# A two-layer adaLN transformer on one core: the second layer's rows, convolution, sort, scatters and combination are put at other places in the order of work

## The chip, the cores and the metric

The program runs on one core of one Trainium2 chip. The core has five engines with a queue each: TensorE (PE, with its weight loads PEld), VectorE (DVE), ScalarE (ACT), GpSimd (POOL) and SyncE (SP), which here only starts transfers. An engine works its queue in order; what it waits for is another engine's result or a transfer. The metric is the device time of one execution in microseconds. The kernel before takes 1100.03 us (median of 3 runs, 1098.54 to 1102.29).

## The reference

Two layers work on x of 4 batches x 1024 rows x 256 columns, float32. In each, x gets a gated attention and then a gated mixture of experts, both on a layer norm that is scaled and shifted by a small modulation of c:

```python
h = _layernorm(x) * (1 + ca) + sa
x = x + ga * attention(h)
h = _layernorm(x) * (1 + cb) + sb
x = x + gb * experts(h)
```

Layer 0 has causal softmax attention (16 heads) and 16 experts with two chosen per row. Layer 1, which the change is about, has linear attention and 8 experts with one chosen:

```python
q, k, v = split(h @ w_qkv.T)                  # 16 heads of 16
q, k = norm(norm(relu(q) + eps) ** 3), norm(norm(relu(k) + eps) ** 3)
out = (q @ (k.T @ v)) / (q @ k.sum(rows) + eps)
conv = depthwise convolution of out over the rows, 3 taps, + b_dwc
attention = (out + conv) @ w_proj.T + b_proj

probs = softmax(h @ router_w + router_b)
experts = max(probs) * (h @ expert_w[argmax] + expert_b[argmax])
```

## The kernel before

All of x stays in SBUF (`k.x[b]`, 8 tiles of 128 rows). Layer 0 is untouched by the change, apart from a combination of its experts' results (`k.awaited`) that runs on into layer 1.

**Attention 1** (`attention1`) loops over b = 0 to 4. In turn b, the generators `front(b)` (norm, keys and values, queries) and `back(b - 1)` (output, convolution, projection, residual) are advanced by one `yield` each, turn by turn. A front takes 18 turns (23 where it computes its own statistics, b = 2 and 3), a back 13. A convolution takes two of them: ScalarE multiplies a 128x1024 half of the channels by the middle tap (L1597), VectorE adds the other two (L1601). Then four turns project (L1609) and add to x (L1614).

After each turn `k.around.step(pieces, rides)` (L44) lets other work in. `tasks` are generators whose yields are costs; `pieces` of cost are advanced per turn, by `pace` in sixths (L1622). `riders` are generators that are advanced `rides` times; they issue GpSimd's indirect transfers one by one. So what is around an instruction is set by the order of these calls. A planner then orders each engine's queue by readiness in that order; instructions given to `k.pin` keep their written order among themselves.

**Experts 1** (`Experts1`) sorts rows by expert. `PARTS` has three parts: batches 0 and 1, batch 2, batch 3. When a batch's back is done, `rows(b)` becomes a task: statistics, the normalised rows in two halves of four tiles (`routed_rows`, L1017; for batches 2 and 3 ScalarE alone does this, and scale and shift come later), a store to DRAM (`rows_in`), transposes, router logits. After a part's last batch, `sort(p)` finds each row's place and each tile's expert; then the rider `send(p)` loads rows (`hs`) and scatters them to `sorted1` with 8 indirect transfers per batch. Each scatter is tied (`paced`, L980) to the matmul that was last issued when it was written.

`run` (L1883) then goes through the pairs of sorted tiles, 11 for part 0 and 7 each for parts 1 and 2: load a pair (`xs`, up to five ahead, six buffers), transpose it (L1923), copy to SBUF (`xT`, L1927, or with scale and shift at L1930), multiply by its expert's weights (L1938), add the bias (L1944), gate (L1946), store to `results`. After each pair `around.step(2, 2)`. When a part's pairs are done, `combine(p)` becomes a task: it gathers result rows back (`ys`, L974, four ahead, six buffers), scales and adds them to x (L2002 to L2008 for part 0, L1996 for the others) and stores four tiles at a time to the output (L2010). Between, `count_sums` checks in three VectorE passes that all sums were in range (its tiles `good` take buffers of `xs`), and `out_of_bounds` reads the flag that decides whether a general version must run.

## Time and profile before

| what | us |
|---|---|
| median of the runs | 1100.03 |
| the profiled execution | 1087.63 |
| its span | 1085.8 |
| TensorE busy | 945.7 (87%) |
| VectorE busy | 620.4 (57%) |
| ScalarE busy | 602.5 (55%) |
| GpSimd busy | 336.0 (31%) |
| mean granted clock of TensorE | 0.955 |

Attention 1 begins at about 750 us of the span. The third turn of its loop (b = 2) is at about 830 to 885, the fourth at 885 to 937 and the fifth, the last back, at 937 to 970. The pairs of the experts follow until 1060. From there to 1085.8 the results of the last part are gathered and stored.

In the lines below, a form such as 128x512 is partitions by elements, x8 a number of instructions merged into one line, and a bracket the idle time of the engine before them with what ended it. A product appears as two records (ps_y x200 for 100 calls), a transpose as one (ps_xT x100 for 100). POOL's DMA_INDIRECT is the time in which GpSimd issues an indirect transfer, not the transfer itself.

### The profile page before, as it was taken

How to read it: one execution, taken by the hardware profiler on the slowest of the kernel's cores; microseconds unless marked ns; L12 is line 12 of the kernel's file. 1: busy time of each engine (PE TensorE's matmuls, PEld its weight loads, DVE VectorE, ACT ScalarE, POOL GpSimd, SP SyncE). 2: the span in 40 equal slices, each digit the busy share in tenths (PEclk: the TensorE clock that was granted, in tenths of full speed). 3: DMA queues.
4: the chain of work that ended last, by engine and by line, in shares of the span. 5: the costliest groups of instructions: out<-in, count | busy, mean ns of one | idle time of the engine just before them, and what ended most of it. 6: DMA issues, size and time to landing. Idle time of an engine off the chain costs nothing.

```text
span 1085.8 us, 18090 instructions
## 1 busy us (share of the span) xinstructions
PE 945.7 (87%) x6072; PEld 559.8 (52%) x6072; DVE 620.4 (57%) x1987; ACT 602.5 (55%) x959; POOL 336.0 (31%) x528
## 2 busy tenths in 40 slices
PE   4899999999999999889679989986997989858760
PEld 2434434443443434335568878874464656547550
DVE  5822235422465155413676767993899968564572
ACT  0368655765477555775555657766654745523430
POOL 2013211311232234663004615612550100553632
PEclk9999999999999999999899999998999899989875
DMA  6995000100010001552825556624223201458764
GB/s 206 358 346 179 1 1 6 40 1 1 1 64 1 1 30 54 201 215 78 317 88 170 197 177 189 196 75 144 67 65 148 88 2 39 141 170 264 240 205 130
DMA packets 97142, 132.89 MB, mean 122 GB/s; under 512 B 8536, under 2 KB 84216, under 8 KB 96528
## 3 DMA queue, kind: packets, MB, share of 16 engines
q1 hardware_dynamic: 84656, 97.27, 26.9%
q0 software_dynamic: 11776, 33.57, 9.9%
q8 instruction: 52, 0.85, 0.3%
q10 hardware_dynamic: 608, 0.79, 0.3%
q14 instruction: 50, 0.41, 0.1%
HBM read 67.85 MB, written 63.75 MB: 121 GB/s over the span
## 4 chain that ended last, share of the span: by engine, by line
PE 63%; DVE 19%; issue 5%; DMA 5%; ACT 4%; POOL 1%; SPq 1%; DVEq 0%; ACTq 0%; POOLq 0%
PE ps_s L388 13%; PE ps_av L453 12%; PE ps_qk L364 6%; PE ps_y L1312 5%; PE ps_h L1247 4%; PE ps_v L349 3%; PE ps_out L427 3%; PE ps_pr L1609 3%; PE ps_y L1938 3%; PE ps_q L1537 2%; PE ps_k L1511 2%; DVE y L1601 2%; DMA ys<-results,index 2%; PE ps_lnT L1057 1%; DVE st L1258 1%
## 5 line engine op out<-in xcount | busy, mean ns | idle before, releaser
L396 ACT ACTIVATE pT<-ps_s 128x1024 f32<-128x1024 f32 x288 | 279.3, 1022 | 169.7 <-PE ps_s L388 167.2
L399 POOL TENSOR_SCALAR_AFFINE_SELECT pT<-pT 128x256 f32<-128x256 f32 x256 | 104.2, 431 | 328.4 <-ACT pT L396 323.7
L388 PE MATMUL ps_s<-qT,kT 32*128 32x512 f32 (+3 forms) x1536 | 178.8, 523 | 0.1
L453 PE MATMUL ps_av<-pT,v 128*32 128x512 f32 (+3 forms) x1536 | 165.2, 497 | 9.4 <-DVE turned L411 5.6
L964 POOL DMA_INDIRECT sorted<-hs,index x96 | 96.2, 1002 | 144.9 <-PE ps_y L1312 73.0
L974 POOL DMA_INDIRECT ys<-results,index x96 | 102.7, 1070 | 119.0 <-DMA results<-y 43.6
L388 PEld LDWEIGHTS ps_s<-qT,kT 32*128 32x128 f32 x1536 | 74.5, 185 | 95.5 <-issue 72.8
L453 PEld LDWEIGHTS ps_av<-pT,v 128*32 128x32 f32 x1536 | 40.6, 108 | 104.0 <-issue 58.7
L1247 PE MATMUL ps_h<-w,xT 128*128 x352 | 82.1, 386 | 6.5 <-DVE mv L1259 3.8
L1312 PE MATMUL ps_y<-w,act 128*128 x352 | 83.7, 392 | 4.2 <-DVE rs_seed L84 2.8
L411 DVE STREAM_TRANSPOSE turned<-ps_av 128x512 f32<-128x512 f32 x32 | 22.8, 712 | 98.9 <-PE ps_av L453 98.6
L1312 PEld LDWEIGHTS ps_y<-w,act 128*128 128x128 f32 x352 | 67.7, 197 | 14.0 <-ACT act L1295 4.8
L1247 PEld LDWEIGHTS ps_h<-w,xT 128*128 128x128 f32 x352 | 66.2, 193 | 15.9 <-issue 4.2
L1295 ACT ACTIVATE act<-ps_hT,gain 128x128 f32<-128x128 f32 x176 | 63.6, 463 | 16.9 <-PE ps_hT L1286 16.8
L1270 ACT ACTIVATE hid<-hid,nmr,rstd 128x256 f32<-128x256 f32 x88 | 47.5, 603 | 39.4 <-DVE nmr L1263 39.2
L1511 PE MATMUL ps_k<-wqkv,hT 128*128 128x512 f32 x128 | 61.9, 603 | 3.6 <-DMA wqkv<-in_wqkv_dram 2.8
L1938 PE MATMUL ps_y<-we,xT 128*128 x200 | 53.0, 412 | 10.6 <-ACT xT L1930 8.4
L371 DVE COPY qT<-ps_qk 128x512 f32<-128x512 f32 x16 | 11.0, 688 | 81.8 <-PE ps_qk L364 81.8
L103 DVE BATCH_NORM_STATS2 ln_st<-x 128x6 f32<-128x256 f32 x128 | 49.2, 407 | 0.5
L1255 DVE TENSOR_TENSOR hid<-ps_h,b 128x256 f32<-128x256 f32 x88 | 33.9, 415 | 26.6 <-PE ps_h L1247 21.5
L1938 PEld LDWEIGHTS ps_y<-we,xT 128*128 128x128 f32 x200 | 38.2, 204 | 20.1 <-ACT xT L1930 11.6
L374 DVE TENSOR_SCALAR kT<-ps_qk,par 128x512 f32<-128x512 f32 x32 | 22.5, 745 | 37.0 <-PE ps_qk L364 37.0
(223 smaller groups left out, 1499.4 us busy)
## 6 DMA issues: line engine op xcount, KB each, us to landing
xs<-sorted SPq DMA_DIRECT2D x69, 256.0 KB, 3.8
results<-y SPq DMA_DIRECT2D x69, 256.0 KB, 3.0
sorted<-zero SPq DMA_DIRECT2D x2, 6016.0 KB, 20.1
rows_in<-h SPq DMA_DIRECT2D x16, 512.0 KB, 2.9
hs<-rows_in POOLq DMA_DIRECT2D x32, 256.0 KB, 3.5
w<-in_w_dram SPq DMA_DIRECT2D x8, 1024.0 KB, 11.3
x<-in_x_dram SPq DMA_DIRECT2D x4, 1024.0 KB, 6.5
b<-in_b_dram SPq DMA_DIRECT2D x2, 2048.0 KB
```

What stands on the lines that cost most here:

```text
L364: nc.tensor.matmul(ps, lhsT=w[:, cc, g * P : (g + 1) * P], rhs=hT[:, cc, hf * 512 : (hf + 1) * 512], start=cc == 0, stop=cc == CC - 1,)
L388: k.anchor = nc.tensor.matmul(pair[hh // 2][:, hh % 2, c0 : c0 + w], lhsT=kTs[o][rows, kb * P : (kb + 1) * P], rhs=qT[rows, q1 - w : q1], ...
L396: nc.scalar.activation(pT, ps, AF.Exp, scale=1.0 / L**0.5)
L399: nc.gpsimd.affine_select(out=pT[:, :, c0 : c0 + P], in_=pT[:, :, c0 : c0 + P], compare_op=ALU.is_ge, fill=0.0, base=0, pattern=[[0, 2], [ ...
L453: nc.tensor.matmul(po[32 * hh : 32 * hh + 32, 512 - w :], lhsT=vs[b % 2][:, kb, 8 * g + 2 * hh + o, :], rhs=exps[b, g, o, u][hh // 2][:, h ...
L964: i = self.k.nc.gpsimd.indirect_dma_start(out=buffer.ap, out_offset=bass.IndirectOffsetOnAxis(ap=index, axis=0), in_=rows, in_offset=None, ...
L974: self.paced(self.k.nc.gpsimd.indirect_dma_start(out=rows, out_offset=None, in_=buffer.ap, in_offset=bass.IndirectOffsetOnAxis(ap=index, a ...
L1247: mm = nc.tensor.matmul(ph[:, j], lhsT=xTs[i // 2][:, j, cc], rhs=w1[:, cc, bass.ds(at[i + j], C)], start=cc == 0, stop=cc == CC - 1,)
L1295: o = nc.scalar.activation(act[:, j, cc], pt[:, j, cc], AF.Gelu, bias=gain[:, 1, cc, t : t + 1], scale=gain[:, 0, cc, t : t + 1],)
L1312: mm = nc.tensor.matmul(po[:, j], lhsT=acts[i // 2][:, j, cc], rhs=w2[:, cc, bass.ds(at[i + j], C)], start=cc == 0, stop=cc == CC - 1,)
L1511: k.anchor = nc.tensor.matmul(ps, lhsT=hT[:, cc, t * P : (t + 1) * P], rhs=wqkv[:, cc, C:], start=cc == 0, stop=cc == CC - 1,).ins
L1938: k.anchor = nc.tensor.matmul(po[:, j], lhsT=xT[:, j, cc], rhs=self.we[:, cc, bass.ds(at[j], C)], start=cc == 0, stop=cc == CC - 1,).ins
```

## The change

- In turn b = 2, the tasks around begin after the first seven turns. The paces of b = 2 and b = 3 go from 6 to 8 and 9. Riders are advanced twice per turn from b = 3 on.
- Where ScalarE normalises alone (batches 2 and 3), both halves are normalised ahead of the transposes.
- The addition of 1 to the middle tap moves from the start of attention 1 to the first back.
- The last back convolves 511 and 513 columns, each as soon as its half of `o` is there, inside two turns that exist already; so it has 11 turns.
- During its turns 6 to 9, four pairs of part 0 are worked on (`beside`), in free buffers of `hT` and in PSUM of the fronts.
- In `run`, 3.5 pieces of the last batch's rows go ahead of the first pair; the rest of rows and sort are spread over the next seven pairs as 0, 2, 3.5, 2.5, 0, 2, 2 pieces. Three rides follow each pair.
- The last part's scatters go to the head of the riders and are not tied to a matmul.
- The gathers are riders of their own, with 24 buffers; the combination of part 0 begins four pairs before the end, the others after all gathers are issued. One more of its instructions is pinned.
- `count_sums` yields after each pass, one pass per pair of part 0; its tiles take the buffers of `out`.

The core of the diff (in the new methods, `tiles_of` is as before, but for the PSUM and SBUF it takes from `k.bank` and `self.space`, and pins on its first transpose, its copies and its first matmul):

```diff
-        good = pool.tile([P, 8 * B * H], F32, tag="xs", name="good", bufs=6)
+        good = pool.tile([P, 8 * B * H], F32, tag="out", name="good")
         count_within(k, good, rec, low, high, k.good[:, i : i + 1])
+        yield
...
-        self.paced(i)
+        if not at_once:
+            self.paced(i)
...
     h = yield from normalised(0)
+    second = (yield from normalised(1)) if scale is None else None
...
+            if b == B - 1:
+                for _ in convolve(o, y, *((0, N // 2 - 1), (N // 2 - 1, N))[q]):
+                    pass
             yield
...
+        if b < B - 1:
+            yield from convolve(o, y, 0, N)
...
-        pace = (6, 8, 6, 6, 12)[b]
+        pace, first = ((6, 0), (8, 0), (8, 7), (9, 0), (12, 0))[b]
         n = 0
+        turn = 0
         while todo:
             todo = [g for g in todo if next(g, k) is not k]
-            n += pace
-            k.around.step(n // 6)
+            turn += 1
+            if turn > first:
+                n += pace
+            k.around.step(n // 6, 1 + b // (B - 1))
             n %= 6
+            if b == B:
+                fill(turn)
...
-        k.around.riders.append(self.send(p, index))
+        k.around.riders.insert(0 if p + 1 == len(PARTS) else len(k.around.riders), self.send(p, index))
...
+    def beside(self, turn):
+        if 0 not in self.sent or turn > 9:
+            return
+        if self.space is None:
+            xs, other = (self.k.spare().rearrange("p c (n d) -> p (c n) d", d=2 * C) for _ in range(2))
...
+            self.space, self.most = space, 4
+        self.fetch()
+        if 6 <= turn <= 9:
+            self.pair()
+        if turn == 9:
+            self.products()
...
+        pieces = [0, 2, 3.5, 2.5, 0, 2, 2] if early else []
+        if early:
+            around.step(3.5, 0)
+        while self.done < len(self.pairs):
...
+            self.pair()
+            if p == 0 and self.done > 6:
+                next(counts, None)
+            if self.done == len(self.pairs) or self.pairs[self.done][0] != p:
+                around.riders.append(self.gathers(p))
+            if self.done == len(self.pairs) - 4:
+                around.tasks.append(self.combine(0))
+            around.step(pieces.pop(0) if pieces else 2, 3)
...
+    def gathers(self, p):
+        index = self.state[p][0]
+        for n in range(self.sortings[p].nt):
+            ys = self.back.tile([P, C], F32, tag="ys", name="ys", bufs=24)
+            self.sortings[p].gather(ys, self.k.results1[p], index[:, 0, n : n + 1])
+            self.got[p].append(ys)
+            yield
```

## The prediction

> **What bounds the kernel now.** I read the busy time by stage first, then what TensorE waits for inside the late stages, then the queues behind those waits, and last the chain of waits at the end. The profiled execution took 1087.63 us (span 1085.8 us). The median of the runs shown is 1100.03 us, 12.4 us (1.1%) more; the sum is made in the profiled execution and its difference is carried over to the median.
>
> The windows by stage (length, then busy us of PE, PEld, DVE, ACT, POOL, granted clock, DMA share, GB/s):
>
> ```profile
> 830.00:884.60 54.60, 45.49 (x215) 29.41 (x216) 48.51 (x165) 31.54 (x60) 3.20 (x8) 0.91 0.30 110
> ```
>
> The line above is the third batch's front beside the second batch's back: VectorE is the fuller engine. The next lines are the last back, then part 0 of the experts, then parts 1 and 2, then the tail.
>
> ```profile
> 936.90:970.20 33.30, 20.72 (x145) 16.85 (x143) 21.35 (x73) 12.95 (x22) 17.80 (x20) 0.85 0.58 186
> 970.20:1005.80 35.60, 30.33 (x189) 23.84 (x188) 16.24 (x73) 13.11 (x25) 15.76 (x19) 1.00 0.80 252
> 1005.80:1048.90 43.10, 28.11 (x127) 22.10 (x126) 30.70 (x62) 17.91 (x38) 25.56 (x24) 0.89 0.73 223
> 1059.70:1085.80 26.10, 0.19 (x2) 0.11 (x2) 6.29 (x16) 0.00 (x0) 8.07 (x8) 0.57 0.43 135
> ```
>
> TensorE is busy 62% of the last back, 85% of part 0, 65% of the stretch after it, and not at all in the tail: the kernel's end is a chain of waits. TensorE's timeline shows where (the bracket is the idle time before and what ended it):
>
> ```profile
> 960.54 8.94 PE L1609 MATMUL ps_pr<-wg,y 128*128 128x256 f32 x32
> ...
> 1013.10 1.89 PE L1938 MATMUL ps_y<-we,xT 128*128 x8
> ...
> 1019.01 3.54 PE L1938 MATMUL ps_y<-we,xT 128*128 x8 [3.58 <-ACT xT L1930]
> ...
> 1027.93 2.83 PE L1938 MATMUL ps_y<-we,xT 128*128 x8 [3.22 <-ACT xT L1930]
> ...
> 1048.90 2.30 PE L1923 MATMUL ps_xT<-ident,xs 128*128 128x128 f32 x8 [6.42 <-DMA xs<-sorted]
> 1051.46 3.75 PE L1938 MATMUL ps_y<-we,xT 128*128 x8 [0.26 <-issue]
> ```
>
> An undisturbed pair's product takes 1.9 us; after an idle gap the same 8 matmuls take 2.8 to 3.8 (the granted clock of 1048.9 to 1059.7 was 0.66). The ACT gaps come from the combination of part 0, whose scalings are pinned ahead of the pairs' evictions and wait for gathers. On ScalarE:
>
> ```profile
> 1014.86 0.51 ACT L2002 ACTIVATE out<-ys,part 128x256 f32<-128x256 f32 x1 [2.64 <-DMA ys<-results,index]
> 1017.24 0.51 ACT L2002 ACTIVATE out<-ys,part 128x256 f32<-128x256 f32 x1 [1.87 <-DMA ys<-results,index]
> ```
>
> The 6.42 us gap is the xs loads. The three `good` tiles share their buffers with xs, and on SP they also stand behind a y that VectorE delivers late:
>
> ```profile
> 1042.89 0.36 SPq L1947 DMA_DIRECT2D results<-y  x1
> 1043.34 1.62 SPq L1008 DMA_DIRECT2D xs<-sorted  x3
> ```
>
> GpSimd's queue gives the end: the last batch's first scatter, the first gather of part 0, the first and last gather of part 2.
>
> ```profile
> 996.40 1.06 POOL L964 DMA_INDIRECT sorted<-hs,index  x1 [8.65 <-PE ps_expert L949]
> ...
> 1010.81 1.04 POOL L974 DMA_INDIRECT ys<-results,index  x1 [4.34 <-PE ps_y L1938]
> ...
> 1065.12 1.00 POOL L974 DMA_INDIRECT ys<-results,index  x1 [14.78 <-DMA results<-y]
> ...
> 1074.33 1.00 POOL L974 DMA_INDIRECT ys<-results,index  x1 [0.31 <-DVE x L1996]
> ```
>
> **The change, part by part.** Call X the end of the last residual add of the last back (970.2 now).
>
> *First rows seven turns later, other paces.* In the 54.6 us stretch TensorE stands 5.72 us (836.4 to 842.1) because VectorE did row 0's statistics (832.2 to 837.0) and its two h products (1.22 + 1.21 us) ahead of the front's ln_nmr at 841.9. Those come after it now: about 5 us earlier for the front. Row 0's work has to go somewhere: VectorE stands only 6 us in the window, and after 857 TensorE is full with ps_k and ps_q, into which 4.4 us of row 0's transposes and routing move. Bounds: -6 (the whole gap) to +4.4 (all of that behind). I take -4, nearest to the gap, since it lies ahead of everything else. The next batch's pace of 9 for 6 brings sort 0 forward (at turn 11 for turn 16 of 23); TensorE has 5.7 us idle in that stretch and VectorE 12.5: 0, between -3 and +3. The scatters of part 0 start at 927.2 now; ten us earlier, and two a turn, 16 scatters and 8 hs loads need what they need now (927.2 to 957.5, 30 us, GpSimd's own pace), so they land at about 949.
>
> *dw's addition moved:* 0.17 us; VectorE waits 8.00 us for dw at 757.6, but the next instruction waits for gate_a1 until 760.15 anyway. 0. *Second normalised half ahead of the transposes* (rows 2 and 3): the same four ACT instructions (2.06 us), nothing added; SP's rows_in store goes out earlier. 0, between -1 and +1.
>
> *Convolution in halves.* Four 1.28 us instructions on VectorE and two of 1.24 on ScalarE become eight and four. The 128x512 form beside (L1492) takes 0.69: 4 x (2 x 0.69 - 1.28) = 0.4 us more on VectorE. Half of the work leaves the path between the last copy of o (951.9) and ps_pr (960.5): -2.8 on VectorE, -1.2 on ScalarE, and the first ps_pr group (2.2 us) can go early: up to -6.
>
> *Four pairs beside it.* A pair is 0.6 us of transposes and 1.9 us of products on TensorE: 4 x 2.5 = 10 us, against 12.6 us idle there. On VectorE 8 x 0.42 = 3.4 us, on ScalarE 4 x 0.59. SP takes four loads and four stores, which stand in its queue with rows 2's rows_in; the loads wait for the 16 scatters (about 949, landing at about 953). The transposes are pinned: if loads are late, the projection is queued behind them. Together with the halves: X between -6 and +8; I take -1, because idle time and added work nearly cancel. So X = 970.2 - 4 - 1 = 965.2.
>
> *The sort over seven pairs, scatters first.* Now X to the first scatter is 26.2 us, with seven pairs' steps of 2; the new steps (3.5 before, then 0, 2, 3.5, 2.5, 0, 2, 2) also end after seven pairs. 26.2 stays (22 to 30): scatter 1 at 991.4. Eight scatters at 1.28 end at 1001.7. They are no longer tied to a matmul, and go ahead of part 0's gathers: that is the new wait. Behind it in GpSimd's queue stand 16 gathers, and for those the combination of part 0, whose pinned scalings now begin four pairs before the end, at about 1010. The first gather lands at about 1006 (1001.7 + 4.2, as at 1013.8 now) and each next tile 1.3 us on, two a pair of 2.2 to 2.5 us: 4 us to spare; if GpSimd is later than that, the ACT gaps come back, and 8.5 us with them.
>
> *Gathers as riders, combinations later, `good` elsewhere.* The ACT gaps go: 3.58 + 3.22 + 1.06 + 0.59 = 8.5 us, and (3.54 - 1.9) + (2.83 - 1.9) = 2.6 of slow clock. The xs gap goes: 6.42 + (3.75 - 1.9) + 1.7 of slow transposes = 10. Four pairs fewer in the run: 35.6 us for eleven is 3.2 each, 13 us. TensorE would end at 1059.7 - 5 - 13 - 11 - 10 = 1021, and part 2's gathers could go 5.4 us later (as now: 1059.7 to 1065.1), at 1026. But GpSimd has 24 gathers before them, at 1.07 + 0.30 = 1.31 to 1.37: 31.5 us after 1001.7 is 1033. **GpSimd becomes what is late next.** From there the tail is as now, 1085.8 - 1065.1 = 20.7: the span ends at 1054, 32 us earlier. The work that now follows the gathers (six tiles of part 0, eight of part 1: 6 x 0.50 on ScalarE, 3 x 1.37 + 8 x 0.48 on VectorE) fits beside part 2's gathers (10.5 us). Two more output stores and part 1's go in the tail too, where the DMA share is 0.43.
>
> *Against it:* transfers are packed tighter, where the share was already 0.80 and 0.73. From 990 on 17.7 MB are left (28 loads and stores of 256 KB, 8 scatters and 32 gathers of 128 KB, 4 MB out, hs); at the 252 GB/s of 970 to 1006 that is 70 us, or 1060. I put 4 us on that (0 to 8). **Sum: -32 + 4 = -28 us**, 1059.6 in the profiled execution, 1072 from the median.
>
> [...] In the rows, gathers beside a VectorE 70% busy took a mean of 1.07 us against a least of 1.00. [...]
>
> **The rivals.**
> (1) *The last back is stretched:* pinned transposes wait for late loads. For it: scatters end 30 us after they start whatever the pace, and 957.5 plus 2.6 plus 4.0 is 964 if sort 0 comes no earlier. Against it: ps_pr waits for the convolution until 960.5 anyway. X at +8 for -1: -19, 1081.
> (2) *The pairs don't move:* the planner puts them behind the projection. The GpSimd chain hangs on X, not on them: -28 + 4 = -24, 1076.
> (3) *GpSimd isn't late:* gathers of part 0 run while the sort is still going. Then TensorE's 1026 holds: 7 us better, 1065; transfers at 252 GB/s speak against it.
> (4) *Slower:* the four pairs run one at a time, each load, transposes, copy, product and addition in series: 4.0 + 1.0 + 0.6 + 2.0 + 0.8 = 8.4 us with the projection behind each, 34 us. It decides when it beats the 28: from three and a half pairs in series, giving 1106. Against it: the loads are issued four at a time, and TensorE has three PSUM buffers for them.
>
> **How the numbers follow.** Forecast 0.55; (1) 0.20; (2) 0.08; (3) 0.07; (4) 0.10. The range takes the forecast, (2), (3) and most of (1): down to 1058 (X at its low end with (3)) and up to 1093 (X +8, sort at 30, transfers +8). A measurement of this kernel tells 0.3%, 3.3 us, from no change. Faster 0.87 (all but (4), and 0.03 of (1) at its worst, which is the same); same 0.03; slower 0.10.
>
> **What would show it.** Right: no ACT gap over 1 us before ps_y, no xs gap; the first scatter of the last batch at about 991; gathers in a row from there to the tail, and part 2's first gather not waiting for its results but for the queue. Wrong: a gap before ps_xT or ps_pr between 945 and 965, results or xs standing on SP behind a load that waits for scatters, gathers at 1.5 us and more, or X later than 975.

## The result and the profile after

The changed kernel takes 1100.22 us (median of 12 runs, 1093.52 to 1103.72) and the kernel before 1098.3 us (median of 12, 1094.31 to 1102.29). The ratio is 1.001, with a 95% interval of 0.9988 to 1.0033: no change that can be measured. Forecast was 1072, a gain of 2.5%.

The kernel before takes about 1098 us in some sets of runs and about 1087 in others, here called a chip of the slow and of the fast kind: its profile (1087.63 us) is an execution of the fast kind, while the result and the profile after (1100.76 us, span 1098.9) are of the slow kind. So stages are compared within a kind. All times below marked "from gate_a1" are counted from the first product with gate_a1 on VectorE (760.15 in the profile before, 771.09 in the profile after). Up to that point the order of work is the same in all these kernels but for the 0.17 us addition to dw, so what differs before it (757 to 767 on the fast kind, 764 to 771 on the slow) is no edit's doing.

| from gate_a1, us | last ps_q | X, last residual add | first scatter of last batch | first gather of part 0 | last product | first gather of part 2 | span's end |
|---|---|---|---|---|---|---|---|
| before, fast kind (the profile before) | 176.8 | 210.1 | 236.2 | 250.7 | 299.5 | 305.0 | 325.6 |
| forecast from it | | 205.0 | 231.2 | 241.5 | 260.9 | 272.9 | 293.9 |
| changed, fast kind | 169.7 | 214.3 | 249.0 | 259.3 | 284.3 | 297.2 | 318.8 |
| before, slow kind | 177.9 | 211.2 | 237.6 | 256.9 | 304.7 | 310.1 | 330.6 |
| changed, slow kind (the profile after) | 170.9 | 214.6 | 249.1 | 260.8 | 295.3 | 305.5 | 327.8 |

On either kind the change gains 7 us up to the last ps_q, loses 10 to 11 in the last back and 8 to 9 from X to the first scatter of the last batch, and gains 14 (slow) or 20 (fast) after it.

The windows of the profile after, by the same stages as those of before, which are of the fast kind (length, then busy us of PE, PEld, DVE, ACT, POOL, granted clock, DMA share, GB/s): third batch's front with the second's back, last back, part 0, parts 1 and 2, tail from part 2's first gather.

```profile
841.00:888.90 47.90, 44.12 (x219) 27.66 (x219) 44.15 (x160) 27.98 (x54) 3.19 (x8) 1.00 0.34 124
942.00:985.70 43.70, 31.22 (x185) 25.73 (x183) 24.30 (x85) 15.61 (x27) 10.64 (x12) 0.88 0.36 120
985.70:1020.15 34.45, 22.96 (x138) 18.65 (x138) 18.94 (x76) 10.85 (x20) 6.50 (x10) 0.85 0.70 222
1020.15:1066.40 46.25, 37.90 (x172) 31.04 (x172) 21.30 (x44) 18.09 (x38) 31.15 (x31) 0.85 0.65 206
1076.60:1098.90 22.30, 0.00 (x0) 0.00 (x0) 7.46 (x17) 0.00 (x0) 9.21 (x8) 0.50 0.54 174
```

The front is full now: TensorE is busy 44.1 of 47.9 us (45.5 of 54.6 before). The last back got longer (43.7 for 33.3) and TensorE does 10.5 us more in it, about what the forecast gave the four pairs (10). Part 0, of 7 pairs for 11, takes 34.5 us for 35.6, with TensorE busy two thirds of it. TensorE's timeline after, in the last back and behind it:

```profile
941.86 1.81 PE L1596 MATMUL ps_o<-kv,qT 128*128 128x136 f32 x12
950.26 0.88 PE L1940 MATMUL ps_xT<-ident,spare 128*128 128x128 f32 x3 [6.59 <-DMA spare<-sorted]
...
967.41 2.48 PE L1957 MATMUL ps_y<-we,spare 128*128 x8 [2.65 <-ACT spare L1946]
...
970.65 2.71 PE L1628 MATMUL ps_pr<-wg,y 128*128 128x256 f32 x8
...
983.05 1.89 PE L1628 MATMUL ps_pr<-wg,y 128*128 128x256 f32 x8
987.57 0.66 PE L1940 MATMUL ps_xT<-ident,xs 128*128 128x128 f32 x4 [2.62 <-DMA xs<-sorted]
...
1020.26 0.20 PE L950 MATMUL ps_expert<-past,all 8*1 8x14 f32 x2 [2.67 <-DVE past L946]
```

The first pair's transposes stand behind only 12 of the 32 ps_o records and wait 6.59 us for rows that the scatters have only just written; ps_pr begins at 970.65. Behind X the xs loads are late. SyncE's queue says why, and ScalarE's what it does to the copies:

```profile
971.79 12.61 SPq L1969 DMA_DIRECT2D results<-spare  x4
984.45 4.17 SPq L1010 DMA_DIRECT2D xs<-sorted  x7
```

```profile
989.11 4.04 ACT L1032 ACTIVATE h<-x,ln_mv,ln_rstd 128x256 f32<-128x256 f32 x8 [8.67 <-DMA xs<-sorted]
993.05 1.04 ACT L1946 COPY xT<-ps_xT 128x512 f32<-128x512 f32 x2
```

The run's loads stand behind the four pairs' last store, and both halves of the last batch's h (eight activations) stand ahead of the first copy of xT, so TensorE gets no product until 993.67. All three come back on the fast kind, in changed_again: 7.29 us of wait before ps_xT, 12.51 us of the four stores, 4.04 us of the eight activations. GpSimd after, the lines that answer to those before:

```profile
1020.15 1.06 POOL L965 DMA_INDIRECT sorted<-hs,index  x1 [20.64 <-DVE past L946]
...
1031.93 1.05 POOL L976 DMA_INDIRECT ys<-results,index  x1 [1.72 <-PE ps_xT L1940]
...
1076.61 1.40 POOL L976 DMA_INDIRECT ys<-results,index  x1 [8.28 <-issue]
...
1086.95 1.00 POOL L976 DMA_INDIRECT ys<-results,index  x1 [0.30 <-DMA ys<-results,index]
```

Two forecasts are seen here: part 0's gathers follow the scatters at once, and ScalarE's waits for ys are gone (its first combination comes at 1055.31). But part 2's first gather does wait, 8.28 us. The row names no releaser; SyncE issues the last two stores of results at 1070.46 to 1072.21, 4.4 us ahead of it, so it is read here as a wait for part 2's results.

### The profile page after: what moved, and what is told of

It is laid out like the page before. It is cut to its first block, busy times and chain, and to the rows that moved or that the text cites. A ratio compares the mean times of both kernels' runs of the same rounds, so it can differ in the third digit from the quotient of the medians.

```text
span 1098.9 us, 18082 instructions
## 1 busy us (share of the span) xinstructions
PE 953.4 (87%) x6072; PEld 565.3 (51%) x6072; DVE 618.2 (56%) x1991; ACT 603.5 (55%) x961; POOL 335.2 (30%) x528
## 4 chain that ended last, share of the span: by engine, by line
PE 65%; DVE 18%; issue 6%; DMA 5%; ACT 4%; POOL 1%; SPq 1%; DVEq 1%; POOLq 0%; ACTq 0%
PE ps_s L388 13%; PE ps_av L453 12%; PE ps_qk L364 5%; PE ps_h L1254 5%; PE ps_y L1319 4%; PE ps_k L1516 3%; PE ps_v L349 3%; PE ps_y L1957 3%; PE ps_out L427 3%; PE ps_pr L1628 2%; PE ps_lnT L1060 2%; PE ps_q L1542 1%; DVE ln_st L103 1%; DVE y L1570 1%; PE ps_xT L1231 1%
## 5 line engine op out<-in xcount | busy, mean ns | idle before, releaser
L965 POOL DMA_INDIRECT sorted<-hs,index x96 | 96.1, 1001 | 169.7 <-PE ps_y L1319 75.8
L976 POOL DMA_INDIRECT ys<-results,index x96 | 102.5, 1068 | 114.0 <-DMA results<-y 32.3
L1319 PE MATMUL ps_y<-w,act 128*128 x352 | 87.0, 403 | 7.8 <-ACT act L1302 4.9
L1957 PE MATMUL ps_y<-we,xT 128*128 x168 | 46.1, 426 | 11.4 <-issue 5.2
L1262 DVE TENSOR_TENSOR hid<-ps_h,b 128x256 f32<-128x256 f32 x88 | 33.9, 415 | 33.2 <-PE ps_h L1254 13.4
L1328 DVE TENSOR_TENSOR y<-ps_y,b 128x256 f32<-128x256 f32 x88 | 35.1, 418 | 19.7 <-PE ps_y L1319 12.1
```

Source lines behind the costliest of these rows:

```text
L965: i = self.k.nc.gpsimd.indirect_dma_start(out=buffer.ap, out_offset=bass.IndirectOffsetOnAxis(ap=index, axis=0), in_=rows, in_offset=None, ...
L976: self.paced(self.k.nc.gpsimd.indirect_dma_start(out=rows, out_offset=None, in_=buffer.ap, in_offset=bass.IndirectOffsetOnAxis(ap=index, a ...
L1319: mm = nc.tensor.matmul(po[:, j], lhsT=acts[i // 2][:, j, cc], rhs=w2[:, cc, bass.ds(at[i + j], C)], start=cc == 0, stop=cc == CC - 1,)
L1957: mm = nc.tensor.matmul(po[:, j], lhsT=xT[:, j, cc], rhs=self.we[:, cc, bass.ds(at[j], C)], start=cc == 0, stop=cc == CC - 1,)
```

## The experiments

Each ratio is to the kernel before on the same chip. The kernel before took 1086.87, 1087.8 and 1086.19 us in three of the sets (fast kind) and 1098.03 and 1098.51 in two (slow kind). In the expectations of the first two sets (the first ten rows but for the last two) times count from the issue of gate_a1's load, 6.4 to 7.0 us ahead of the product; the measured times here are all "from gate_a1". The stages of the fast kind, then of the slow kind:

| from gate_a1, us | last ps_q | X | first scatter | first gather of 0 | last product | first gather of 2 | end | ratio, 95% interval |
|---|---|---|---|---|---|---|---|---|
| before_good | 176.6 | 209.6 | 235.8 | 250.4 | 291.7 | 305.2 | 325.8 | 1.0014 (0.9997 to 1.0032) |
| late_part_only | 177.8 | 210.7 | 236.6 | 256.7 | 282.4 | 293.9 | 315.8 | 0.9905 (0.9879 to 0.9932) |
| changed_again | 169.7 | 214.3 | 249.0 | 259.3 | 284.3 | 297.2 | 318.8 | 0.9945 (0.9923 to 0.9967) |
| pairs_later | 173.2 | 214.8 | 249.5 | 259.9 | 286.2 | 298.1 | 320.5 | 0.9930 (0.9911 to 0.9949) |
| no_beside | 173.3 | 206.8 | 237.3 | 258.6 | 284.5 | 296.4 | 317.9 | 0.9925 (0.9905 to 0.9944) |
| even_sort | 169.9 | 214.3 | 246.6 | 257.0 | 283.8 | 295.7 | 317.2 | 0.9912 (0.9888 to 0.9937) |
| even_no_beside | 169.9 | 202.0 | 230.9 | 251.9 | 277.6 | 289.0 | 311.2 | 0.9864 (0.9837 to 0.9892) |
| combine_last | 170.0 | 214.3 | 247.4 | 257.7 | 281.5 | 291.3 | 314.9 | 0.9874 (0.9846 to 0.9902) |
| best_third | 173.2 | 207.6 | 233.7 | 254.7 | 280.8 | 288.8 | 311.9 | 0.9872 (0.9845 to 0.9899) |
| gathers_after | 172.9 | 207.4 | 233.4 | 280.9 | 280.6 | 314.6 | 335.6 | 1.0082 (1.0055 to 1.0109) |
| slow: before_again | 177.9 | 211.2 | 237.6 | 256.9 | 304.7 | 310.1 | 330.6 | 1.0005 (0.9973 to 1.0036) |
| slow: late_part_again | 177.6 | 210.9 | 237.0 | 258.4 | 300.3 | 309.2 | 331.4 | 1.0049 (1.0024 to 1.0073) |
| slow: changed_third | 171.0 | 214.8 | 249.5 | 261.3 | 299.8 | 306.8 | 328.7 | 0.9972 (0.9956 to 0.9988) |
| slow: early_data | 171.4 | 208.2 | 243.0 | 254.7 | 293.0 | 300.5 | 322.2 | 0.9935 (0.9910 to 0.9960) |
| slow: even_no_beside_again | 170.9 | 204.5 | 230.2 | 251.5 | 293.0 | 302.3 | 324.4 | 0.9984 (0.9960 to 1.0008) |
| slow: best | 170.9 | 204.5 | 230.3 | 251.6 | 295.7 | 302.2 | 326.8 | 0.9974 (0.9955 to 0.9992) |
| slow: best_again | 171.2 | 205.4 | 234.1 | 255.4 | 296.2 | 303.1 | 327.5 | 0.9978 (0.9951 to 1.0006) |
| slow: best_counts_later | 170.7 | 204.9 | 233.3 | 253.1 | 300.9 | 306.9 | 331.5 | 0.9956 (0.9928 to 0.9984), of 7 of 12 executions; see its text |

A last ps_q at 173 for 170 (no_beside, pairs_later, best_third, gathers_after) is no edit's doing: no_beside and the changed kernel order all work up to it alike, and in no_beside a group of ps_k in the front took 4.54 us where changed_again has 2.84. So the last back is read as X less the last ps_q. A row of stages is one execution, the ratio is of several: the profile of no_beside is the longest of its six (1086.47 us, median 1078.75), those of even_sort and pairs_later are the longest of theirs, by 3.2 us over the median each.

### Without the four pairs: no_beside

```diff
     def beside(self, turn):
-        if 0 not in self.sent or turn > 9:
-            return
+        return
```

> The changed kernel without the four pairs beside the last back; all eleven pairs of part 0 follow it. Times are counted from the landing of gate_a1's load, and X is the end of the last residual add (216.6 before, 221.4 after, span's end 332.2 and 334.7). Theory A (TensorE stands 6.6 us because the pairs' pinned transposes wait for their loads, and the last back is queued behind them): the gap goes, X is at 211 to 213, 9 us earlier, and the four pairs come back behind X at 2.5 to 3.2 us each, so the end is between 2 us earlier and 4 later than the changed kernel's 1100. Rival B (the last back is longer because second halves, sort and rows of batches 2 and 3 now lie in it): X stays at 219 to 222 and the time is 10 us longer, about 1110.

The gap is gone and X comes 33.5 us after the last ps_q, for 44.6 in changed_again: 11 us earlier (7.5 from gate_a1). The end is 317.9 for 318.8. That is theory A's picture as a whole, and B's +10 us is out. What leaving the pairs out gains in the last back, eleven pairs behind X pay back. But this run doesn't say whether the pairs' wait or their work stretches the back; the next two do.

### The pairs ordered behind ps_o: pairs_later

```diff
                 if j == cc == 0:
                     k.pin(tr)
+                    if self.most == 4:
+                        self.sortings[p].paced(tr.ins)
```

> The changed kernel with one order added: the transposes of the four pairs beside come after the last back's product of kv and qT that was issued last (no other work moves by hand). Theory A: the products and transposes of the last back no longer stand behind the loads, X comes 6 to 9 us earlier (212 to 215) and so does the end, 1092 to 1094. Rival B: X within 2 us of 221.4 and the time the same. Rival F (what was saved waits elsewhere, since the fourth store of the four pairs still holds the next loads on SP): X 6 us earlier, the wait for xs behind it longer by as much, the time the same.

X is 41.6 us after the last ps_q and, from gate_a1, at 214.8 for 214.3: theory A's 6 to 9 us did not come, the number is B's. TensorE's timeline of pairs_later shows where they went:

```profile
949.10 0.66 PE L1940 MATMUL ps_xT<-ident,spare 128*128 128x128 f32 x4
...
955.95 0.66 PE L896 MATMUL ps_rank<-sel,before 128*128 128x64 f32 x2 [4.70 <-DVE part L1890]
956.40 0.64 PE L896 MATMUL ps_rank<-sel,all 128*128 128x64 f32 x2
956.83 3.73 PE L1628 MATMUL ps_pr<-wg,y 128*128 128x256 f32 x8
960.48 0.20 PE L950 MATMUL ps_expert<-past,all 8*1 8x14 f32 x2
960.69 1.09 PE L1940 MATMUL ps_xT<-ident,spare 128*128 128x128 f32 x4
961.57 2.06 PE L1959 MATMUL ps_y<-we,spare 128*128 x8
963.46 1.89 PE L1628 MATMUL ps_pr<-wg,y 128*128 128x256 f32 x8
```

The wait for loads is gone, and ps_pr starts 22.9 us after the last ps_q (956.83 - 760.78 - 173.2) for 28.7 in the profile after (970.65 - 771.09 - 170.9). But TensorE now stands 4.70 us for VectorE ahead of the projection, and the products of all four pairs lie between the projection's groups (three pairs in the profile after). Idle time and the pairs' work lie in the same stage, one behind the other.

### The same pairs with rows that are there: early_data

```diff
-            self.k.sorted1[p].load(xs[:, : len(tiles)], tiles)
+            if self.most == 4:
+                self.k.nc.sync.dma_start(xs, self.k.rows_in[0].part(tiles))
+            else:
+                self.k.sorted1[p].load(xs[:, : len(tiles)], tiles)
```

> The changed kernel, but the four pairs beside the last back are loaded from the rows of batch 0 as they were written, which no scatter holds, and not from the sorted rows; so these four pairs compute other rows (part of the output is not the reference's). TensorE's instructions keep their order. The loads land some 10 us earlier. Theory A (the wait of the pinned transposes is what stretches the last back): no gap over 1 us before ps_xT at the head of the last back, the last residual add (X) 6 to 9 us earlier after the last ps_q than the 44.6 us of the changed kernel, so 36 to 38, and the time 0.5% shorter. Theory O (the four pairs' own 10 us of TensorE stand between the projection's groups, and the waits move): X 42 to 45 us after the last ps_q, the time within 0.2%.

X is 36.8 us after the last ps_q, for 43.8 in changed_third on the same chip: 7.0 us, as theory A had it. The ratio is 0.9935 for 0.9972. TensorE's timeline of early_data, for the first lines of the profile after:

```profile
935.15 1.81 PE L1596 MATMUL ps_o<-kv,qT 128*128 128x136 f32 x12
936.80 0.49 PE L1943 MATMUL ps_xT<-ident,spare 128*128 128x128 f32 x3
937.22 0.70 PE L1596 MATMUL ps_o<-kv,qT 128*128 128x136 f32 x4
```

So with TensorE's order unchanged, the wait for scattered rows is worth 7 us of the 11. (These four pairs compute other rows, so part of this kernel's output is not the reference's.) Only rows that are there in time let the pairs fill the idle time ahead of the projection; an order that avoids the wait (pairs_later) moves the pairs out of that time and gains nothing in X.

### The sort as before: even_sort

```diff
-        pieces = [0, 2, 3.5, 2.5, 0, 2, 2] if early else []
-        if early:
-            around.step(3.5, 0)
+        pieces = []
...
-    second = (yield from normalised(1)) if scale is None else None
+    second = None
```

> The changed kernel with the last batch's row statistics, second normalised half and sort as before: two pieces after every pair, nothing ahead of the first, the second half normalised after the first one's transposes. Theory C (these two hold the last batch's first scatter back): X stays at 221, from X to the first scatter of the last batch 26 to 28 us for 34.5, the end 7 to 8 us earlier, 1092. Rival D (the sort ends with VectorE's and TensorE's other work whatever its pieces): 33 to 36 us and the same time. Rival E (GpSimd or the transfers set the end): the scatter comes 7 us earlier and the end moves by less than 2.

X stays and the scatter comes 32.3 us after it, for 34.7: theory C's 26 to 28 was not reached, and rival D's 33 to 36 is nearer. The ratio is 0.9912 for 0.9945, on another chip of the same kind. So the spread sort and the early second half together cost 2.4 us here (and 1.6 against combine_last's 33.1). The rest can be read from the table: from X to the scatter it is 26.1 before, 25.9 in late_part_only, 25.7 to 28.9 in the six executions with the even sort and no pairs, 30.5 in no_beside (spread sort, no pairs), 32.3 and 33.1 with the even sort and the pairs, 34.5 to 34.8 with the pairs and the spread sort. So the pairs are the larger part, 3 to 7 us. That fits what SyncE's queue showed, their stores ahead of the run's loads, but no run takes those stores alone away. The early second half and the spread pieces were not separated either: in even_sort the first product behind X comes 4.5 us after it for 8.0 in changed_again, and yet the last batch's router logits end at the same distance (22.2 and 22.4 us), so the wait of the first copies is not what holds the sort.

### Both undone: even_no_beside

> The changed kernel without the four pairs beside the last back and with the sort's pieces and second half as before (both undone). Theory C (the sort holds the last batch's scatter, the pairs hold X): X at 213, the first scatter 26 to 28 later at 240, the end 3 to 5 us earlier than with either one alone, 319 to 321, 1073. Rival K (eleven pairs behind X set the first gather of part 0 at 265, and 24 gathers in a row and part 2's eight follow): first gather at 264 to 266, end 323 to 325, 1078.

X at 202.0, 12.3 us earlier than with the pairs (32.1 us behind the last ps_q), the scatter at 230.9, the end at 311.2 and the ratio 0.9864 (C's 319 to 321 from the load are 312 to 314 in this count). Theory C's sum holds, and K's reason shows too: the first gather comes 21.0 us after the first scatter, 10.7 more than the scatters need, since eleven pairs of part 0 now lie ahead of it. The pairs beside cost this kernel 6.0 us (317.2 to 311.2); with the combination last it is 3.0 (combine_last 314.9, best_third 311.9), and there the two ratios are the same, 0.9874 and 0.9872. The pairs buy an early first gather relative to X, but not an early one.

### The late part by itself: late_part_only

The kernel before with the changed run; from the changed kernel it differs by the edits of even_no_beside and by

```diff
-        pace, first = ((6, 0), (8, 0), (8, 7), (9, 0), (12, 0))[b]
+        pace, first = ((6, 0), (8, 0), (6, 0), (6, 0), (12, 0))[b]
-            k.around.step(n // 6, 1 + b // (B - 1))
+            k.around.step(n // 6)
...
-            if b == B - 1:
+            if b == B:
...
-        if b < B - 1:
-            yield from convolve(o, y, 0, N)
+        yield from convolve(o, y, 0, N)
```

> The kernel before with the changed run alone: gathers as riders into 24 buffers, the combination of part 0 four pairs before the end, the last part's scatters first, the sums' bounds spread over pairs and in the buffers of out; the paces, the first rows, the whole convolution, the eleven pairs behind it and the even sort stay as before. Theory G' (the late part's gain is real and its own): X at 216 to 217, no wait over 1 us on ScalarE's xT or on xs before a product, last product at 294 to 297, end 324 to 328, ratio 0.99. Rival L (the gain of the variants is the earlier X alone): end 330 to 333, ratio 1.00.

X and the scatter are those of before; the last product comes 17.1 us earlier, at 282.4 (expected 287 to 291 in this count), and the end 9.8 us earlier. There is no wait over 0.3 us before a product in parts 1 and 2. G' holds: on the fast kind the late part alone gains 0.95%, and the changed kernel as a whole gains less, 0.55%.

### One line of it: before_good

```diff
-        good = pool.tile([P, 8 * B * H], F32, tag="xs", name="good", bufs=6)
+        good = pool.tile([P, 8 * B * H], F32, tag="out", name="good")
```

> The kernel before with one line of the change: the three tiles of the sums' bounds take the buffers of out and not of xs. Theory G (the 6.42 us wait for xs and the slow clock after it come from these tiles' buffers): no wait for xs over 1 us in parts 1 and 2, the end 6 to 10 us earlier, 1088 to 1092. Rival H (the load stands on SP behind a late store of y, or the end hangs on GpSimd's queue): the wait becomes another one in the same place, or the tail waits, and the time stays within 3 us of 1098.

The 6.42 us wait for xs is gone and the last product comes 7.8 us earlier (291.7 for 299.5), and the end does not move: rival H. The last product ends at 1050.28; VectorE's last addition of a y starts 7.4 us behind that, among the combination of part 1 and the passes over the sums, and SyncE's last stores and GpSimd's first gather of part 2 follow it:

```profile
1055.95 0.48 DVE L1996 SCALAR_TENSOR_TENSOR x<-ys,part,x 128x256 f32<-128x256 f32 x1 [1.19 <-DMA ys<-results,index]
...
1057.69 0.42 DVE L1944 TENSOR_TENSOR y<-ps_y,be 128x256 f32<-128x256 f32 x1
...
1058.14 0.69 DVE L1946 TENSOR_TENSOR y<-y,gate_f 128x512 f32<-128x512 f32 x1
```

```profile
1057.80 1.42 SPq L1947 DMA_DIRECT2D results<-y  x2
```

```profile
1063.80 1.00 POOL L974 DMA_INDIRECT ys<-results,index  x1 [11.75 <-PEq L2114]
```

### The combination last: combine_last, best, best_third

```diff
-            if self.done == len(self.pairs) - 4:
+            if self.done == len(self.pairs):
                 around.tasks.append(self.combine(0))
...
         while around.riders:
-            around.step(0)
+            around.step(1)
```

> The kernel of the even sort with the combination of part 0 started after the last pair and not four pairs before it. There part 2's first gather came 12 us after TensorE's last product, for 5.5 in the kernel before, with 8 products of the combination (1.4 us a tile pair with their additions) on VectorE among the last pairs' additions. Theory M (these hold the last store): 5 to 7 us from the last product to the first gather of part 2, the end 4 to 6 us earlier than the even sort's 323.6, 1073. Rival N (the combination then stands behind the gathers, in the tail): the gather earlier, the tail from it 25 us and more for 21.5, and the same time.

combine_last has this on top of even_sort. Part 2's first gather comes 9.8 us after the last product for 11.9, the end 2.3 us earlier, the ratio 0.9874 for 0.9912: M's direction at half its size. Now the gather before it starts only 1.3 us ahead (290.0 and 291.3), so GpSimd's own queue is the bound, which the prediction had named (even_sort ran on another chip of the same kind). best adds it to even_no_beside:

> Without the four pairs, with the even sort, and with the combination of part 0 after the last pair: the three edits that each gained, together. If their gains are of different waits (X, the last scatter, VectorE ahead of the last store), counted from the first product with gate_a1: first gather of part 0 at 251 to 253, 24 in a row to 284, part 2's first at 284 to 285 (for 289.0 without the last edit), end 306 to 308, ratio 0.982. Rival K (the queue of 24 gathers in a row hides the earlier store): part 2's first gather at 285 or later and the ratio no better than 0.986.

> Without the pairs, even sort, combination of part 0 last, once more for a chip of the fast kind: there end 306 to 308 and ratio 0.982. On the slow kind as twice before: 0.997 to 0.998.

best met the slow kind (0.9974), best_third the fast one: 311.9 and 0.9872, no better than even_no_beside's 0.9864. Rival K holds: 32 gathers stand in a row from 254.7 on, and an earlier store finds the queue full. The best version measured is even_no_beside, 1.4% under the kernel before on the fast kind (with combine_last and best_third inside its interval), and no different from it on the slow kind (0.9984).

> As best, with the passes over the attention's sums beside the first three pairs of part 1 and not beside the last four of part 0. Theory P (these passes, 2.2 us of VectorE each, stand between the links of the last batch's sort): from X to the first scatter of the last batch 26 us for 28.9, the first gather of part 0 the same 252 (the last result of part 0 holds it), the time within 0.2% of best. Rival Q (VectorE is the bound of parts 1 and 2): the last product and the end 2 to 4 us later than best.

Its edit takes the passes over the sums from part 0's last four pairs to part 1's first three. From X to the first scatter it shows 28.4 us, no less than best's 25.8 to 28.7, so nothing speaks for P; the last product is 5 us later, which speaks for Q. But its times scatter from 1085.43 to 1104.28: the seven shortest of twelve give the ratio 0.9956, while the median of all twelve is 1100.62 for 1098.03 before, so no verdict rests on it.

### The changed kernel again: changed_again, changed_third

> The changed kernel itself, beside the others. Times are counted from the load of gate_a1. Theory I (the waits of 3.76 and 2.06 us before products of parts 1 and 2, and the slow clock after them, belong to its order of work): they return, the last product ends at 300 to 303, the ratio to before is 1.00. Theory J (they belong to that one execution): the last product ends at 290 to 293 as in the kernels with one part undone, the span's end is 324 to 327 and the ratio 0.99.

> The changed kernel once more, as a control beside these: its ratio to before was 1.001 in one set of runs and 0.9945 in another. If the difference is in the chip, this one is near one of the two and the stage of parts 1 and 2 goes with it: last product at 284 (ratio 0.994) or 295 (ratio 1.00) after the first product with gate_a1.

0.9945 on a chip of the fast kind, 0.9972 on one of the slow kind, 1.001 in the result. The last product comes at 284.3, 299.8 and 295.3. Theory J, but by the kind and not by the single execution: the waits and the late last product come back on the slow kind and not on the fast one. The ratios on the slow kind don't follow this stage, though: the later last product (299.8) has the better ratio (0.9972).

### The slow kind: before_again, late_part_again and the others

> The kernel before, profiled beside the others on one chip, times counted from the first product with gate_a1. Its profile so far came from a chip where it takes 1087; on the chips of the first and third sets it takes 1098. If this chip is of the fast kind: last product 299 to 300, end 325 to 326. If it is of the slow kind: theory R (engines stand without a recorded releaser wherever transfers are dense, in any kernel): such waits of 2 us and more in its parts 1 and 2 too, end at 329 to 332. Theory S (only the changed order of the late part is hit): none, end 326, and the slow kind's 11 us lie in the first layer.

> The kernel before with the changed run alone. Fast kind: as measured, end 316, ratio 0.9905. Slow kind: theory R' (the late part's gain of 10 us is what the waits without a releaser eat): last product at 290 to 296 for 282, end 322 to 326, ratio 0.996 to 1.001. Theory S' (the loss on the slow kind is the attention's): ratio 0.99 there too.

> The same with the combination four pairs before the end. Fast kind: as measured, end 311, ratio 0.986. Slow kind: if the loss there grows with how tightly parts 1 and 2 are packed, 0.990 to 0.997 with the waits; if it comes from the combination behind the gathers only, 0.986 here too.

> Without the pairs, even sort, combination of part 0 last. On a chip of the fast kind (before 1087): end 306 to 308, ratio 0.982, 4 us under the same kernel with the combination four pairs before the end. On a chip of the slow kind (before 1098): as measured there, end 325 to 328 and ratio 0.997, with waits without a recorded releaser on ScalarE and VectorE of 15 us in all in parts 1 and 2.

This chip was of the slow kind. Theory R: the kernel before has such waits too. Its last product comes 5.2 us later than on the fast kind, its end 5.0. Theory R': the late part alone, 0.9905 on the fast kind, is 1.0049 here, beyond the theory's own range of 0.996 to 1.001; its last product comes at 300.3 for 282.4. even_no_beside_again, at 0.9984, met neither of its two forecasts (0.990 to 0.997, or 0.986); best_again, at 0.9978 with its end at 327.5, met the one for the slow kind. The sums of ScalarE's waits in the late stages of before_again, late_part_again and best_again, one line each (us in total, times, longest):

```profile
ACT xT L1927 <- remote: 6.3, 1, 6.3
```

```profile
ACT xT L1948 <- remote: 16.6, 3, 7.7
```

```profile
ACT xT L1949 <- remote: 19.4, 4, 9.1
```

"remote" is a release that the profile can't name. The windows of ten us of best (slow kind) and, for the same stage, of even_no_beside (fast kind) show that the DMA engines weren't full:

```profile
1024.00:1034.00 10.00, 1.97 (x6) 1.47 (x5) 1.54 (x3) 1.02 (x2) 7.87 (x8) 0.62 0.58 169
```

```profile
1022.30:1032.30 10.00, 9.73 (x55) 8.32 (x54) 6.96 (x14) 5.69 (x13) 7.72 (x8) 1.00 0.91 276
```

In the first of them TensorE is busy for 1.97 us, VectorE for 1.54 and ScalarE for 1.02, and GpSimd goes on with its gathers at the same pace (8 in either, 7.87 and 7.72 us); the DMA share is 0.58 where the other has 0.91. A single late transfer is not ruled out by that.

> Without the pairs and with the even sort, and all 32 gathers and the combinations tied to TensorE's last product, so that no gather and no combination runs beside parts 1 and 2. Counted from the first product with gate_a1. On a chip of the slow kind: theory U (the engines stand because gathers run beside them): no wait without a releaser over 2 us before the last product, which comes at 275 to 279 as on the fast kind, for 293. Theory V (they stand by the density of the loads and stores, or by the chip): they remain, last product at 285 or later. On the fast kind this says nothing of them; last product at 275 to 278. In both the end is 25 to 35 us later than with the gathers beside.

```diff
-                around.riders.append(self.gathers(p))
+            if self.done == len(self.pairs):
+                around.riders += [self.gathers(q) for q in range(last + 1)]
```

gathers_after ran on a chip of the fast kind, so U and V stay untried. What it shows there: with no gather beside it the last product comes at 280.6, as in best_third beside 24 gathers (280.8), so the gathers did not slow the products there; and 32 gathers put behind the last product cost 24 us (335.6 for 311.9; 25 to 35 were expected).

## Why the prediction was wrong, point by point

The forecast's sum, -28 us, was made in an execution of the fast kind, so changed_again is its measure: -6.8 us there (325.6 to 318.8). Its end was forecast at 293.9, without the 4 us laid on for dense transfers. The 24.9 us between fall into these steps.

**"First rows seven turns later, other paces": -4 taken, -7 measured** to the last ps_q (176.8 to 169.7). Right in its mechanism, and too small by 3, more than the whole gap of 6 that it counted: with row 0's work away, TensorE's front has hardly a gap. The scatters of part 0 started 16.9 us earlier (150.1 for 167.0), more than the "ten us" of the text, and took 24.1 us and not the 30 that they "need", so they ended 23.2 earlier (174.2 for 197.4).

**"Together with the halves: X between -6 and +8; I take -1".** This step failed first: it set added work against idle time and put the wait of the pinned transposes at nothing in its sum. From the last ps_q to X it is 44.6 us for 33.3: +11.3, outside its own bounds, and its sign of being wrong, a gap before ps_xT, is there with 7.29 us, some ten us earlier than it was looked for. The forecast compared 10 us of pair work with 12.6 us of idle time and let one fill the other. early_data shows that 7.0 are the wait for the scattered rows, which rival (1) had named and priced at X +8; no_beside shows the rest, since without pairs the back is 33.5. The halves of the convolution, forecast at up to -6, gained 1.2 us at the most (32.1 to 34.5 in the kernels without pairs, for 33.3 before). "the loads wait for the 16 scatters (about 949, landing at about 953)" was the line that held the answer: the transposes, pinned ahead of 20 of the 32 ps_o records, took everything behind them on TensorE into that wait. X as a whole is +9.3 against the forecast.

**"26.2 stays (22 to 30)": 34.7, +8.5.** The step that failed second. The forecast counted pieces and pairs (seven and seven), and left out what stands ahead of them: SyncE's queue, where four stores of 12.6 us hold the run's first loads, and ScalarE's, where eight activations for h stand ahead of the first copies. Moving the second half ahead was taken as 0, because "the same four ACT instructions" run; what it costs was not measured by itself. Of the 8.5 the spread of the sort and the early second half together make about 2 and the pairs 3 to 7; which of the pairs' own steps makes those is argued from SyncE's queue and not shown.

**Scatters and gathers in a row: right.** The first gather comes 10.3 us after the first scatter, to the tenth as forecast. 24 gathers take 33.9 us (259.3 to 293.2, the last start and 1.3), for 31.5; that sum had used the shorter of its two steps, 1.31, and 1.37 gives 32.9.

**"GpSimd becomes what is late next": wrong by 4.** It comes 5.3 us after the start of the one before it, and waits for the results. TensorE had not ended at 261 but at 284.3, since X and the sort were late, and VectorE held the last additions among the combination of part 0: from the last product to the gather 12.9 us for the 5.4 that the forecast took over. In combine_last and best_third, where the combination is out of the way, GpSimd's queue is indeed what is late (the gather before it starts 1.3 us ahead in both).

**The waits that go: right.** ScalarE's for ys and TensorE's for xs in parts 1 and 2 are gone (none in the profile after), and so, on the fast kind, are the slow products behind them: eight matmuls of a product take 1.9 to 2.0 us in best_third, for 2.8 to 3.8 behind the gaps before (in the profile after, 3.5 and 3.3 behind its waits of 3.76 and 2.06). late_part_only, which has this part of the change without the others, gains 9.8 us. The sum of 8.5 + 2.6 + 10 for TensorE was near (17.1 in its last product), but before_good shows that a gap closed on TensorE isn't one closed at the end: 7.8 us there gave none.

**The tail:** 21.6 for 20.7. **Gathers at 1.07 us: right.** The mean of the last 32 is 1.068 us before, 1.064 in the profile after, 1.105 in changed_again and 1.156 at the most (best_third), which over the least of 1.00 is 5 us in all; a mean of 1.5, the forecast's sign of being wrong, is in none of them.

**"1072 from the median":** the 12.4 us between execution and median were carried over as a constant. They are near the difference between the two kinds (1086 to 1088 and 1098), and part of it lies in the very stages that were changed: 5.0 us in the kernel before, 9.0 in the changed one (318.8 to 327.8), 15.6 in the late part alone (315.8 to 331.4). Of the 0.55% gained on the fast kind, 0.28% is left in changed_third and nothing in the result.

**The rivals.** (1) was right in its mechanism, and its X +8 is what came, though not for the reason it gave: the scatters ended 23 us earlier, and the pinned transposes came up before them all the same. It alone doesn't give the result, since the sort and the last store add 12 us more. (2) and (3) fell: the planner left the pairs where they were put, and GpSimd's queue ran in a row. (4), pairs in series, holds in part: three of the four stand between the projection's groups.

## What to carry to other kernels

Idle time in a stage is room for other work only at the moments at which that work's data is there (7.0 us of the last back went to rows that were not): compare times of arrival, not sums, and where the inserted instructions are pinned, add their wait to everything queued behind them on the same engine. A step that adds no instruction can still hold up another, by standing ahead of it in a queue (here four stores of 12.6 us ahead of the run's loads, eight activations of 4.0 us ahead of the first copies): for a store, a copy or a half moved forward, read who is next on SyncE and ScalarE. Closing an engine's gap shortens the kernel only if the path to the end goes through it (in before_good the last product came 7.8 us earlier and the end did not); here the same late additions on VectorE and then GpSimd's queue took over twice.

## What the runs showed of the hardware that was not expected

The kernel before takes 1086 to 1088 us in three of the sets of runs and 1098 in the three others, with nearly the same granted clock in the profiles (0.955 and 0.949). Five of the sets are on five different chips and the sixth names none; no chip was measured twice, so whether the chip or the occasion decides is not shown. On the slow kind ScalarE, VectorE and TensorE stand at the same time in parts 1 and 2 (busy for 1.0, 1.5 and 2.0 of ten us in best; a single wait of ScalarE's is up to 9.8 us, in even_no_beside_again) while GpSimd goes on, with no release that the profile names; on the fast kind ScalarE's waits in parts 1 and 2 of the profile before, changed_again, late_part_only, best_third and gathers_after hold none. On ScalarE they sum to 6.3 us in the kernel before, 10 to 17 in early_data, changed_third, even_no_beside_again and late_part_again, and 19 to 24 in best, best_again and best_counts_later, so mostly more where the later stages were packed more; but two executions of the same changed kernel have 4.8 (the profile after) and 11.1. The traces of the slow kind also hold fewer records of events (8,910 to 9,030 semaphore updates for 11,750 to 11,790, of the same work), and in the late stages half are missing: 715 landings of transfers between X and the last product in before_again, 1,452 in the profile before. So a release without a name may be one whose record is missing, and only the standing itself is shown. What holds the engines there was not found. A change whose gain is in such a stage has to be measured on more than one chip: the late part alone is 0.9905 on one and 1.0049 on another, both with intervals that exclude 1.
